# Attention stage: the rows' turns queued behind the experts' last product on VectorE, and a pause of 1024 columns ahead of the experts' down products

## The chip, the cores and the metric

The kernel runs on one core of a Trainium2 chip. The metric is the device time of one launch in microseconds (us). The engines are called PE (TensorE, matrix products), DVE (VectorE), ACT (ScalarE), POOL (GpSimd) and SP (SyncE, which here only issues transfers). Each works through its own queue in order, and semaphores order the queues among each other.

## The reference

Four residual blocks are applied to x, 8 batches of 512 rows of 256 values, all in float32: a scan block, a mixture of experts, an attention, and the same mixture again.

```python
x = x + scan(layernorm(x))         # silu(x Win), a decaying scan over the rows, Wout
x = x + ffn(layernorm(x))          # 16 routed experts, 4 chosen per row, and 2 shared experts
x = x + attention(layernorm(x))    # causal, 16 heads of 16, scores clipped to -10..10
x = x + ffn(layernorm(x))
# within ffn:
sh = jax.nn.silu(x @ sh_gate_w) * (x @ sh_up_w) @ sh_down_w
return (routed + sh).reshape(hidden_states.shape)
```

The change concerns the third block, and the shared experts and the routing of the fourth, which run beside it.

## The kernel before, in words

The kernel has four stretches. From 0 to about 366 us it runs the scan over the batches, with the routing and the shared experts of the first mixture beside it; from there to 746 us the routed experts of the first mixture, in blocks of 128 rows; from 746 to about 1260 us the attention over the batches, with the routing and the shared experts of the second mixture beside it; from there to 1672 us the routed experts of the second mixture. The change touches the third stretch alone.

That stretch is a loop over the batches b = 0 to 7 (`stretch`, with `class Attention`). The work of one pass is cut into pieces, and `beside` traces them interleaved: it always takes the next step of the piece that is furthest behind, by the share of its columns that are done; at a tie the piece that stands first. The pieces of a pass are:

- **main**, the attention of batch b: ten steps. Step n issues a burst of scores (PE, `ps_a`, L1244; three bursts ahead of its use, so that the last bursts belong to batch b+1), whose exponentials ACT takes (L1254) and whose clamps DVE makes (L1264 and L1265), and then a burst of mixing products (PE, `po_a`, L1280). After steps 2, 4, 7 and 9 DVE divides the sums and turns them (L1295 to L1305). Step 9 mixes first, and its score burst follows as a step of its own. Four output products (`py_a`, L486) end the piece. In a middle pass it has 18432 columns.
- **fill**: the projections of batch b+1 (four `pq_a` products, L1192, and four `pv_a`, L1210; 6144 columns) and, from pass 2 on, behind them the shared experts of batch b-2 (`shared_experts`; 12288 columns). These are four rounds of a gate product and an up product (`pg_m`, L1108, 1024 columns each), and four down products (`pd_m`, L1137). Of each round ACT takes a tanh (L1122), and DVE makes two products (L1123 `sig_m`, L1124 `act_m`). The down products read all four `act_m`.
- **pieces by the clock of the pass** (`timed`): a step is due at a given share of the pass. They are the norm, the scores and the choices of batch b-1's routing (the choices L656 to L700 are a long chain of small DVE instructions), the sending of routed rows (POOL), and, for batch b+2, its load, its sum (L166), its norm and its turn.

The turn of batch b+2 goes by `by_shares`: the normed rows `xn` are written to memory and read back by quarters (SP, L416 and L419), and two DVE transposes (L428, `xT_l<-xn`) make the operand of that batch's projections, which are in the next pass. Its two steps are due at `turns = (0.65, 0.85)`: the transfers at 0.65 and the transposes at 0.85.

Tracing order is not queue order. A scheduler orders each engine's queue at build time by its own model of time: an instruction that is traced later goes ahead where it is ready sooner. `tc.issue_after(ins)` takes that freedom away: what is traced within it is queued behind `ins` on the engine of `ins`, without waiting for its result.

In the last pass (b = 7) the shared experts of batch 5 are split: six steps (`HELD`) go into the pass, at an even pace worked out from `columns // 12`, and the rest goes into the piece that follows.

Of the kernel before, what the change touches and what calls it, by code (L numbers as in the profile page):

```python
# [12 lines left out]
ALU = mybir.AluOpType  # L13
# [3 lines left out]
SQ = 32  # L17
QUAD = P // SQ
B, T, D = 8, 512, 256
NT = T // P  # L20
KD = D // P
# [8 lines left out]
NSH = 2  # L30
KF = F // P
# [28 lines left out]
KB, COLS = 9, 6  # L60
HALVED = 1597463007.0
PACE = 2
SENT = 4
HELD = 6
AHEAD = 6
# [17 lines left out]
def tile_hybrid_block(  # L83
# [22 lines left out]
    nc = tc.nc  # L106
# [8 lines left out]
    def bank(shape, name: str, kind: str = "one"):  # L115
        kind = instead.get(kind, kind)
        return stage[kind].tile(shape, FP, tag=kind, name=name)
# [33 lines left out]
    def rows_of(part, b: int):  # L151
        return part[b * T : (b + 1) * T, :].rearrange("(t p) d -> p t d", p=P)
# [139 lines left out]
    steps = const.tile([P, NJ], FP, name="steps")  # L292
# [72 lines left out]
    def timed(steps, *places):  # L365


        def scaled():
            now = 0
            for place in places:  # L370
                yield place - now
                now = place
                next(steps)
            for _ in steps:
                pass

        return Piece(1, scaled())

    def spread(first: float, last: float, many: int):
        return [first + (last - first) * k / many for k in range(many)]  # L380

    def some(steps, many: int):

        for _ in range(many):
            yield next(steps)
# [3 lines left out]
            pass  # L389


    wide = []

    def turned(src, tag: str, into, copies, home=None, past=None):

# [15 lines left out]
    def by_shares(src, tag: str, into, into_rows: bool):  # L411


        rows = src()
        through = dram.tile([T, D], FP, name=f"through_{tag}")
        nc.sync.dma_start(out=through.rearrange("(t p) d -> p t d", p=P), in_=rows)  # L416
        share = rows.rearrange("p t d -> p (t d)") if into_rows else kb4(f"share_{tag}").rearrange("p t d -> p (t d)")
        for a in range(QUAD):
            nc.sync.dma_start(  # L419
                out=share[a * SQ : (a + 1) * SQ, :].rearrange("s (g c) -> s g c", g=T // SQ),  # L420
                in_=through[:, a * KD * SQ : (a + 1) * KD * SQ].rearrange("(g s) c -> s g c", s=SQ),
            )
        yield 0
        dst = work.tile([P, KD, T], FP, tag="kb4", name=f"xT_{tag}", bufs=KB)
        into(dst)
        for half in range(2):
            g = slice(half * T // SQ // 2, (half + 1) * T // SQ // 2)
            nc.vector.transpose(  # L428
                dst.rearrange("p k (g s) -> p k g s", s=SQ)[:, :, g],
                share.rearrange("p (g i k) -> p k g i", i=SQ, k=KD)[:, :, g],  # L430
            )
        yield 0

    by_both = (nc.scalar.copy, nc.vector.tensor_copy)
# [40 lines left out]
    def kb4(name: str):  # L475
        return work.tile([P, NT, D], FP, tag="kb4", name=name, bufs=KB)
# [21 lines left out]
    class Scan:  # L498
        mixture, ahead, copies, turns = 0, 1, by_scalar, (0.75, 0.79)
# [82 lines left out]
    class Route:  # L582
# [24 lines left out]
        def scores(self, shares: bool = False):  # L607
            if shares:
                yield from by_shares(
                    lambda: self.held["rows"][:, :, 0:D], self.tag, lambda xnT: self.held.update(xnT=xnT), False  # L610
                )
                yield from logits(self.i, self.b, self.tag, self.held)
                return
            yield from turned(
                lambda: self.held["rows"][:, :, 0:D],
                self.tag,
                lambda xnT: self.held.update(xnT=xnT),
                self.copies,
                past=wide if self.i == 0 and self.b == B - 2 else None,
            )  # L620
            yield from logits(self.i, self.b, self.tag, self.held)
# [31 lines left out]
    def choices(i: int, b: int, tag: str, held, paced: bool):  # L653
# [96 lines left out]
        for t in range(NT):  # L750
            for k in range(TK):
                at = t * TK + k
                if paced and at % PACE == 0:

                    pair = slice(at, at + PACE)
                    tc.keep_in_program_order(nc.scalar.copy(slots[:, pair], places[:, pair]))  # L756
# [336 lines left out]
    def shared_experts(i: int, b: int, xnT_of, tanh: bool):  # L1093

        tag = f"m{i}_{b}"

        def steps():
            xnT = xnT_of()
            acts = []
            for n in range(NSH):  # L1100
                _, g_sb, u_sb, _ = shared[n]
                act = work.tile([P, KF, T], FP, tag="kb4", name=f"act_{tag}_{n}", bufs=KB)
                acts.append(act)
                for f in range(KF):
                    pair = [bank([P, T], f"pg_{tag}_{n}_{f}_{which}") for which in range(2)]
                    for dst, w in zip(pair, (g_sb, u_sb)):
                        for k in range(KD):
                            made = nc.tensor.matmul(  # L1108
                                dst,
                                lhsT=w[:, k, f * P : (f + 1) * P],  # L1110
                                rhs=xnT[:, k, :],
                                start=(k == 0),
                                stop=(k == KD - 1),
                            )
                        wide[:] = [made]
                        if dst is pair[0]:
                            yield KD * T
                    ph, pu = pair
                    sig = work.tile([P, T], FP, tag="col", name=f"sig_{tag}_{n}_{f}", bufs=COLS)
                    if tanh:  # L1120

                        nc.scalar.activation(sig, ph, AF.Tanh, scale=0.5)  # L1122
                        nc.vector.scalar_tensor_tensor(sig, sig, 1.0, ph, ALU.add, ALU.mult)  # L1123
                        nc.vector.scalar_tensor_tensor(act[:, f, :], sig, 0.5, pu, ALU.mult, ALU.mult)  # L1124
                    else:
                        nc.scalar.activation(sig, ph, AF.Sigmoid)
                        nc.vector.tensor_mul(sig, ph, sig)
                        nc.vector.tensor_mul(act[:, f, :], pu, sig)
                    yield KD * T
            y_sb = kb4(f"ys_{tag}")  # L1130
            for half in range(2):
                py = bank([P, 2, D], f"pd_{tag}_{half}")
                for j in range(2):
                    t = 2 * half + j
                    for n in range(NSH):
                        for f in range(KF):
                            nc.tensor.matmul(  # L1137
                                py[:, j, :],
                                lhsT=acts[n][:, f, t * P : (t + 1) * P],
                                rhs=shared[n][3][:, f, :],  # L1140
                                start=(n == 0 and f == 0),
                                stop=(n == NSH - 1 and f == KF - 1),
                            )
                    yield NSH * KF * D
                nc.scalar.copy(y_sb[:, 2 * half : 2 * half + 2, :], py)

            (nc.gpsimd if b == B - 1 else nc.sync).dma_start(out=rows_of(parts[i][1], b), in_=y_sb)

        return Piece(NSH * KF * (2 * KD * T + NT * D), steps())

# [8 lines left out]
        return w_all[:, at : at + NT * D].rearrange("p (a b) -> p a b", a=rows)  # L1161

    class Attention:
        mixture, ahead, copies, turns = 1, 2, by_both, (0.65, 0.85)
        early = 2
        norms, scores, choose = (0.0, 0.12, 0.2, 0.28), (0.29, 0.45, 0.55, 0.6), (0.66, 0.95)
        last_rows, last_scores = (0.2, 0.28), (0.35, 0.38)
# [212 lines left out]
    def stretch(layer):  # L1380
# [12 lines left out]
        def turn(b: int, copies=layer.copies):  # L1393
            if i == 1 and b >= layer.ahead:
                return by_shares(lambda: xn.pop(b), f"l{i}_{b}", lambda xnT: xT.update({b: xnT}), True)
            return turned(lambda: xn.pop(b), f"l{i}_{b}", lambda xnT: xT.update({b: xnT}), copies)
# [8 lines left out]
        def experts(b: int):  # L1405
            return shared_experts(i, b, lambda: routes.pop(b).held["xnT"], i == 1)
# [37 lines left out]
        for b in range(1 if begun else 0, B):  # L1444
# [19 lines left out]
            if b > 0:  # L1464
# [7 lines left out]
                if last:  # L1472
                    pieces += [
                        timed(r.scores(), *layer.last_scores, *spread(0.5, 0.56, NT)),
                        timed(some(r.rest, PICKS), *spread(0.57, 0.67, PICKS - 1), 0.76),
                        timed(some(r.rest, 3 + SENT), 0.79, 0.81, 0.83, *spread(0.85, 1.0, SENT)),
                    ]
# [17 lines left out]
            if i == 0 and b == 2:  # L1495
# [11 lines left out]
                timed(r.norm(by_vector=True), *spread(0.0, 0.05, 2 * NT)),  # L1507
                timed(sends.pop(), *spread(0.0, 0.5, NT * TK - SENT)),
                timed(r.scores(), 0.2, 0.22, *spread(0.28, 0.33, NT)),
# [111 lines left out]
```

## Time and profile before

| | |
|---|---|
| time, median of 3 runs | 1681.23 us (1679.09 to 1684.41) |
| the profiled execution | 1674.03 us |
| its span, first to last instruction | 1672.1 us |
| PE busy in the span | 1572.9 us, 94% |
| DVE, ACT, POOL busy | 1159.7, 745.4, 758.1 us |
| attention stretch, 746 to 1260 us | PE 479.9 of 514 us busy, DVE 397.3, ACT 222.5, POOL 156.9 |
| mean granted PE clock | 0.977 |

A profile shows one execution. Times in it are counted from the first instruction. A line of the timeline gives the start, the duration, the engine, the source line, the operation and its tiles, how many instructions were merged, and in brackets for how long the engine had been idle and what it had waited for. The granted clock is the share of full speed that PE was given in a window.

### The profile page before, as it was taken

To read this page: it belongs to the slowest core of one execution; us is meant where nothing else is said; L and a number is where in the kernel's file an instruction comes from. 1 tells how busy PE (TensorE), PEld (TensorE's weight loads), DVE (VectorE), ACT (ScalarE), POOL (GpSimd) and SP (SyncE) were. 2 spreads that over 40 slices of the span, in tenths; PEclk is the share of its full clock that TensorE was granted. 3 is DMA by queue.
4 is the path that set the end of the run, shared out by engine and by line. 5 is a ranking of instruction groups with operands and counts; after the bars stand their busy time and mean duration, and the time that the engine had idled before them with its cause. 6 is when DMAs were issued, how large, how long until landed. Compare 5 with 4: busy or idle time off the path is not lost.

```text
span 1672.1 us, 34224 instructions
## 1 busy us (share of the span) xinstructions
PE 1572.9 (94%) x9992; PEld 1156.6 (69%) x9992; DVE 1159.7 (69%) x3623; ACT 745.4 (45%) x1461; POOL 758.1 (45%) x655
## 2 busy tenths in 40 slices
PE   6999996979999999999999999999787999999996
PEld 3566663659999999984444454454356999999996
DVE  7988876436677766656888978978754566666664
ACT  3222332125555555546544443444213555555553
POOL 3365663525555555550023423422552555555554
PEclk9999998989999999999999999999899999999998
DMA  5354431527777766641333423332643767777776
GB/s 166 127 192 170 135 110 60 186 75 106 107 124 122 104 99 99 99 57 42 89 93 107 121 85 117 96 96 90 210 170 72 110 113 113 137 136 136 134 135 133
DMA packets 281645, 195.31 MB, mean 117 GB/s; under 512 B 168592, under 2 KB 262064, under 8 KB 281456
## 3 DMA queue, kind: packets, MB, share of 16 engines
q1 hardware_dynamic: 228368, 119.40, 27.9%
q0 software_dynamic: 51984, 72.09, 23.9%
q8 instruction: 85, 1.39, 0.3%
q10 hardware_dynamic: 1104, 1.57, 0.3%
q14 instruction: 104, 0.85, 0.2%
HBM read 89.71 MB, written 103.23 MB: 115 GB/s over the span
## 4 chain that ended last, share of the span: by engine, by line
PE 38%; DVE 9%; DMA 3%; issue 1%; ACT 1%; another core or an unknown queue 0%; DVEq 0%; POOLq 0%; SPq 0%; ACTq 0%
PE ph L994 13%; PE pyr L1025 6%; PE ps_a L1244 4%; PE pd_m L1137 3%; DMA part<-rows 3%; PE pq_a L1192 2%; PE po_a L1280 2%; PE pg_m L1108 2%; PE py_a L486 2%; PE pv_a L1210 1%; DVE w_all L1264 1%; DVE w_all L1265 1%; DVE act_m L1124 1%; ACT w_all L1254 1%; DVE sig_m L1123 1%
## 5 line engine op out<-in xcount | busy, mean ns | idle before, releaser
L1035 POOL DMA_INDIRECT part<-rows x272 | 426.3, 1567 | 339.7 <-ACT rows L1034 252.3
L759 POOL DMA_INDIRECT xg<-sorted_m,slots_m x256 | 258.6, 1010 | 293.7 <-ACT slots_m L756 78.0
L994 PEld LDWEIGHTS ph<-rows,gate 128*128 128x128 f32 x2160 | 277.8, 191 | 33.4 <-ACT rows L977 21.6
L994 PE MATMUL ph<-rows,gate 128*128 128x128 f32 x2160 | 291.5, 278 | 1.9 <-ACT rows L977 1.9
L994 PE MATMUL ph<-rows,up 128*128 128x128 f32 x2160 | 285.3, 275 | 0.0
L1025 PE MATMUL pyr<-w_all,rows 128*128 x1088 | 279.2, 380 | 0.0
L967 DVE COPY up<-w_all 128x512 f32 x270 | 118.8, 441 | 211.4 <-PE ph L994 191.6
L994 PEld LDWEIGHTS ph<-rows,up 128*128 128x128 f32 x2160 | 262.9, 192 | 0.0
L967 ACT COPY gate<-w_all 128x512 f32 x270 | 166.5, 618 | 122.3 <-DVE up L967 55.7
L1254 ACT ACTIVATE w_all<-ps_a 128x1024 f32<-128x1024 f32 x160 | 155.2, 1021 | 108.5 <-PE ps_a L1244 101.0
L1025 PEld LDWEIGHTS pyr<-w_all,rows 128*128 128x128 f32 x1088 | 186.9, 192 | 14.3
L1034 ACT ACTIVATE rows<-pyr,gain 128x256 f32<-128x256 f32 x272 | 128.9, 474 | 80.9 <-PE pyr L1025 60.1
L1002 ACT ACTIVATE rows<-ph 128x256 f32<-128x256 f32 x272 | 104.6, 384 | 114.3 <-PE ph L994 99.5
L1004 DVE TENSOR_TENSOR rows<-ph,rows 128x256 f32<-128x256 f32 x272 | 115.1, 423 | 31.7 <-ACT rows L1002 27.7
L1005 DVE TENSOR_TENSOR rows<-ph,rows 128x256 f32<-128x256 f32 x272 | 115.2, 424 | 26.2 <-issue 0.9
L1137 PE MATMUL pd_m<-sd_sb,act_m 128*128 128x256 f32 x512 | 122.8, 386 | 7.8 <-DVE act_m L1124 7.7
L1108 PE MATMUL pg_m<-xT_m,sg_sb 128*128 128x512 f32 x256 | 123.3, 604 | 0.0
L1108 PE MATMUL pg_m<-xT_m,su_sb 128*128 128x512 f32 x256 | 122.5, 600 | 0.0
L1137 PEld LDWEIGHTS pd_m<-sd_sb,act_m 128*128 128x128 f32 x512 | 96.4, 192 | 31.3 <-DVE act_m L1124 9.3
L1244 PE MATMUL ps_a<-w_all 32*128 32x384 f32 (+3 forms) x1024 | 104.7, 475 | 14.0 <-ACT w_all L1254 13.9
L1264 DVE SCALAR_TENSOR_TENSOR w_all<-w_all,causal 128x512 f32<-128x512 f32 (+1 forms) x160 | 91.8, 574 | 33.3 <-ACT w_all L1254 31.2
L1244 PEld LDWEIGHTS ps_a<-w_all 32*128 32x128 f32 x1024 | 45.2, 190 | 69.6 <-ACT w_all L1254 39.1
(213 smaller groups left out, 1960.3 us busy)
## 6 DMA issues: line engine op xcount, KB each, us to landing
rows<-xg SPq DMA_DIRECT2D x720, 32.0 KB
rows<-xg SPq DMA_DIRECT2D x92, 134.0 KB
part<-x SPq DMA_DIRECT2D x16, 512.0 KB
part<-ys_m SPq DMA_DIRECT2D x14, 512.0 KB
sum<-part SPq DMA_DIRECT2D x14, 512.0 KB
w_all<-in_L_ffn_gate_w_dram SPq DMA_DIRECT2D x27, 256.0 KB
w_all<-in_L_ffn_up_w_dram SPq DMA_DIRECT2D x27, 256.0 KB
w_all<-in_L_ffn_down_w_dram SPq DMA_DIRECT2D x27, 256.0 KB
```

Source lines behind the costliest of these rows:

```text
L759: nc.gpsimd.indirect_dma_start(out=xg[i], out_offset=bass.IndirectOffsetOnAxis(ap=slots[:, at : at + 1], axis=0), in_=rows[:, t, :], in_of ...
L967: copy(here, w_all[:, bass.ds(held[n][0] + half * KD * F, KD * F)])
L994: nc.tensor.matmul(ph[s][:, f * P : (f + 1) * P], lhsT=both[s][:, k * F + f * P : k * F + (f + 1) * P], rhs=rows[:, ROW + k * P : ROW + (k ...
L1004: nc.vector.tensor_mul(act, ph[0], act)
L1005: made = nc.vector.tensor_mul(act, ph[1], act)
L1025: nc.tensor.matmul(py, lhsT=act[:, f * P : (f + 1) * P], rhs=w_all[:, bass.ds(w + 2 * KD * F + f * D, D)], start=(f == 0), stop=(f == KF - 1),
L1034: nc.scalar.mul(y, py, gain[:, TK : TK + 1])
L1035: acc = nc.gpsimd.indirect_dma_start(out=parts[i][n % 2], out_offset=bass.IndirectOffsetOnAxis(ap=rows[:, D + 2 * TK : D + 2 * TK + 1].bit ...
L1108: made = nc.tensor.matmul(dst, lhsT=w[:, k, f * P : (f + 1) * P], rhs=xnT[:, k, :], start=(k == 0), stop=(k == KD - 1),)
L1137: nc.tensor.matmul(py[:, j, :], lhsT=acts[n][:, f, t * P : (t + 1) * P], rhs=shared[n][3][:, f, :], start=(n == 0 and f == 0), stop=(n == ...
L1244: nc.tensor.matmul(ps[j // 2][:, j % 2, col : col + n], lhsT=k_sb[w][r, o, c * P : (c + 1) * P], rhs=q_sb[r, o, c * P : T], start=True, st ...
L1254: nc.scalar.activation(es[two], ps[two], AF.Exp, scale=ATT_SCALE)
```

## The change

Three edits, all in the attention stretch:

- `shared_experts` pauses for 1024 columns (`BREAK`) between its last `act_m` and its first down product, where it uses tanh (the second mixture). In the pause it traces nothing, and `beside` counts the columns as done. The piece's columns grow from 12288 to 13312, so each of its other steps stands at a smaller share of the fill.
- It keeps its latest `act_m` in `acted`, and the two transposes of the turn (`into_rows`, which is the turn of a later batch) are queued behind it on DVE, once there is one (from pass 2 on).
- The transposes are due at 0.96 of the pass in place of 0.85.

```diff
+BREAK = 1024
...
-    wide = []
+    wide, acted = [], []
...
-            nc.vector.transpose(
-                dst.rearrange("p k (g s) -> p k g s", s=SQ)[:, :, g],
-                share.rearrange("p (g i k) -> p k g i", i=SQ, k=KD)[:, :, g],
-            )
+            with tc.issue_after(acted[-1].ins) if into_rows and acted else nullcontext():
+                nc.vector.transpose(
+                    dst.rearrange("p k (g s) -> p k g s", s=SQ)[:, :, g],
+                    share.rearrange("p (g i k) -> p k g i", i=SQ, k=KD)[:, :, g],
+                )
...
-                        nc.vector.scalar_tensor_tensor(act[:, f, :], sig, 0.5, pu, ALU.mult, ALU.mult)
+                        acted[:] = [nc.vector.scalar_tensor_tensor(act[:, f, :], sig, 0.5, pu, ALU.mult, ALU.mult)]
...
+            if tanh:
+                yield BREAK
             y_sb = kb4(f"ys_{tag}")
...
-        return Piece(NSH * KF * (2 * KD * T + NT * D), steps())
+        return Piece(NSH * KF * (2 * KD * T + NT * D) + tanh * BREAK, steps())
...
-        mixture, ahead, copies, turns = 1, 2, by_both, (0.65, 0.85)
+        mixture, ahead, copies, turns = 1, 2, by_both, (0.65, 0.96)
```

## The prediction

> **What bounds the kernel now.** I read the page's busy shares first, then busy time by stretch, then PE's waits in the attention stretch, then its timeline around each wait. In that stretch PE is busy for 480 of 514 us, so only a stall of PE or a change in its clock moves the end. Its waits from 746 to 1160 us (in total, how often, the longest):
>
> ```profile
> PE pd_m L1137 <- DVE act_m L1124: 7.7, 4, 1.9
> PE ps_a L1244 <- ACT w_all L1254: 4.9, 9, 1.4
> PE py_a L486 <- DVE oT_a L1305: 1.4, 2, 0.7
> ```
>
> The first line is what the change is about: in passes 2 to 5, the down products wait for the experts' last product on DVE. Pass 2, PE:
>
> ```profile
> 893.82 1.98 PE L1108 MATMUL pg_m<-xT_m,sg_sb 128*128 128x512 f32 x4
> 895.64 1.88 PE L1108 MATMUL pg_m<-xT_m,su_sb 128*128 128x512 f32 x4
> 897.45 1.07 PE L1280 MATMUL po_a<-w_all,v_a 128*32 128x128 f32 x16
> 898.45 1.56 PE L1137 MATMUL pd_m<-sd_sb,act_m 128*128 128x256 f32 x6
> 901.93 0.70 PE L1137 MATMUL pd_m<-sd_sb,act_m 128*128 128x256 f32 x2 [1.92 <-DVE act_m L1124]
> ```
>
> Six of the first eight down products need only the first three `act_m`; the fourth is wanted at 901.93 - 1.92 = 900.01. On DVE at that time:
>
> ```profile
> 897.85 0.71 DVE L428 STREAM_TRANSPOSE xT_l<-xn 128x512 f32<-128x512 f32 x1
> 898.48 0.65 DVE L1264 SCALAR_TENSOR_TENSOR w_all<-w_all,causal 128x512 f32<-128x512 f32 x1
> 899.04 0.42 DVE L1265 TENSOR_SCALAR w_all<-w_all 128x512 f32<-128x512 f32 x1
> 899.38 0.71 DVE L428 STREAM_TRANSPOSE xT_l<-xn 128x512 f32<-128x512 f32 x1
> 900.01 1.06 DVE L689 CAST sorted_m<-which_m 128x16 f32<-128x16 uint32 x1
> 900.05 1.02 DVE L1123 SCALAR_TENSOR_TENSOR sig_m<-sig_m,pg_m 128x512 f32<-128x512 f32 x1
> 901.19 0.69 DVE L1124 SCALAR_TENSOR_TENSOR act_m<-sig_m,pg_m 128x512 f32<-128x512 f32 x1
> ```
>
> No line carries an idle time: DVE is late, not waiting. It works from 873.88 to 901.88 with one hole of 0.32 us. Both turns stand ahead of the last product, and each takes 0.63 us to the next start. So does a cast that takes 1.06 us, where its like in pass 6 takes 0.15; it falls on POOL's memset of the value tile (899.96 to 901.03).
>
> After the stall PE's clock is not always whole (the column before the last two is the granted clock):
>
> ```profile
> 902.00:906.00 4.00, 4.00 (x29) 3.06 (x30) 3.62 (x9) 2.20 (x3) 0.00 (x0) 1.00 0.01 2
> 962.50:966.50 4.00, 3.83 (x21) 2.56 (x22) 2.75 (x8) 1.10 (x2) 0.00 (x0) 0.62 0.00 0
> ```
>
> The same stall leaves the clock whole in passes 2 and 4 and drops it in passes 3 and 5. There the score burst that follows takes 2.02 and 2.09 us in place of 1.15, and the next down products 2.75 and 2.57 in place of 1.99: 1.63 + 1.52 = 3.15 us. From one such last product to the next it is 60.74, 62.38 and 60.74 us, and the 62.38 holds pass 3's drop, which agrees. The most that can be had at this place is 7.7 + 3.15 = 10.8 us, 0.64% of the time.
>
> **Part 1: the turns go behind the last product.** 2 x 0.63 = 1.26 us leave the queue ahead of it. The next projections need the operand at 914.54, some 12 us after the old end of the last product, so the turns stay hidden; lost cover would cost that wait at the head of the next pass. Behind `act_m` come the shares of the attention: the turned output ends at 904.51 and the output products start at 905.47. One turn fits into that 0.96 us, and two would cost 0.3 a pass if nothing else moved back. No transfer moves: the step at 0.65 stays, and with it SP's queue and POOL's. Each `xn` is freed some 4 us later; the sum that a later load feeds is 40 us away.
>
> **Part 2: the turns due at 0.96.** From pass 2 on, the new edge already holds them. In passes 0 and 1 there is no `act_m` yet; their turns (800.21, 846.29) run just ahead of the output products' two waits of 0.63 and 0.74. Those could go (-1.4), but in the old due order these turns stood behind the shares too and ran early because they were ready. I take 0.
>
> **Part 3: the pause.** In pass 2 to 6 the fill grows from 18432 to 19456 columns beside a main piece of 18432. Before, most steps of the fill tie with a step of main and come second. Now they come a little earlier and go first: the first gate product goes ahead of the burst of step 4, the second up ahead of step 6, the third up ahead of step 7, the fourth gate ahead of step 8. The first down product moves from 0.778 to 0.789 and stays behind step 9's mixing and ahead of the next score burst (0.833). So a score burst comes to stand between the last gate and the last up product, but between the last up and the first down product there remains the one mixing of 1.07 us.
>
> What that does to DVE: step 4's burst starts 1.82 us later (one gate product, 873.66 to 875.48), and its clamps can start at 875.70 in place of 873.88. Into the hole that this leaves goes the first `sig_m` (0.59). The work up to the last product is 28.00 - 0.32 - 1.26 - 0.59 = 25.83 us, so it ends at 875.70 + 25.83 = 901.53, which is 1.5 us after 900.01; without the cast's 0.91 us it is 0.6. If the rest of the choices (L692 and L700, 0.76) goes ahead as well, because the last product is ready later than they are, it is 2.3. If the choices from L570 on (3.7 us) go behind it, it is 0. **I take a stall of 1.3 in place of 1.92: 4 x -0.6 = -2.4 us** (from -7.7 to +1.4).
>
> **Clock**: a stall of 1.45 us (835.39) was followed by a clock of 0.57, waits of 0.6 and 0.7 by none below 1.00. I let one of two drops go: -1.6 (from -3.15 to +3.15, where the other two passes drop as well).
>
> [...]
>
> **The bursts' own wait.** Two bursts share two buffers, which ACT's two exponentials free. At 785 us a burst ended at 786.35 and the next was held until 2.07 us later, over a mixing of 1.07: stalls of 0.16 + 0.42. Between the bursts of steps 2 and 3 there stood a mixing (0.57) and a `pq_a` (1.98); now there stands a `pv_a` of 0.93. The second starts 1.5 us after the first, runs a quarter (0.27) and waits 0.3 us: 5 passes, **+1.5** (from 0 to 5 x 0.58 = 2.9).
>
> **Pass 6** has no turns. Its last product ended at 1145.88 and was wanted at 1144.63 + 1.56 = 1146.19. With step 6's clamps 1.91 us later (behind the second up product), the 14.7 to 15.5 us of DVE work that follow end at 1146.3 to 1147.2: +0.5 (from 0 to 1.7). Pass 7 changes its order by one product; I take 0.
>
> [...]
>
> **Sum**: -2.4 - 1.6 + 1.5 + 0.5 = -2.0 us. The profiled execution took 1674.03 (span 1672.1 and 1.93 around it), so 1672.0 for one like it; it lies 7.2 under the median of the runs, 1681.23, which becomes **1679.2**.
>
> **Rivals.**
>
> A, the forecast: the stalls shrink and the new order gives most of it back. For it: DVE has no hole from 873.88 to 901.88, so taking out 1.26 us can't remove 1.92 by itself. 1676.2 to 1686.3 (0.3% of 1681.23 is 5.0 us, about what a measurement of this kernel can tell from no change). Chance 0.47.
>
> B, the last product gets clear: the choices go behind it or the cast misses the memset, all four stalls and both drops go. -7.7 - 3.15 + 1.5 = -9.4: 1671.8. With the waits of passes 0 and 1 gone, 1670.4. For it: without turns, pass 6 was on time by 0.31 us. Against: its cast was 0.9 us shorter, and the new order delays the clamps. Chance 0.35.
>
> C, **slower**: DVE's backlog grows. The mechanism is the score bursts that now stand behind a product: their clamps reach DVE 1.8 us later and all stand ahead of the last product. It decides once the work ahead of that product grows by more than the 1.26 us taken out. At 2.3 us a stall: 4 x 0.36 = +1.4; drops in the other two passes, +3.15; pass 6, 1.7 and a drop of 1.6; bursts, 2.9: +10.7, 1691.9; half of it, 1686.6. Chance 0.18.
>
> That the change doesn't do what it says (the edge holds what was harmless) would give A's middle without the gain, +2.0: 1683.2, within A.
>
> **Chances**: faster by over 0.3% is B, 0.35; within, A, 0.47; slower, C, 0.18. The range goes from B with the early waits gone (1670.4) to C a little past its half (1688): 1670.4 to 1688.
>
> **What would show it.** PE's wait for `act_m` in passes 2 to 5: gone (B), 0.6 to 1.5 (A), over 1.9 (C). A wait for ACT ahead of step 3's burst of about 0.3 in passes 2 to 6. The gate product ahead of the burst of step 4, and both turns behind the last `act_m`. The granted clock in the 4 us after the first down products. The cast's duration, and what now falls on the memset. I am wrong if the length of a pass changes by over 1.5 us, or if the time moves in a stretch that the change doesn't touch.

## The result and the profile after

The changed kernel takes 1684.95 us (median of 20 runs) beside 1680.76 for the kernel before on the same chip: a ratio of 1.0025, 95% interval 1.0017 to 1.0033. It is slower by 4.2 us, where 2.0 us less had been forecast. On another chip, where the kernel before takes 1634 us, the ratio is 1.0041 (1.0029 to 1.0053).

The two profiled executions lie 12.9 us apart (1687.18 and 1674.03), more than the medians do: the one of before is 7 us under its median, and 3.4 us of the difference lie ahead of the attention, where the code is the same. From there to the start of pass 1 it takes 60.93 us in place of 59.51: the granted clock fell to 0.62 and 0.53 on the way (766 to 770 and 770 to 774 us), as it does in another execution of the kernel before (e5 below: 0.72 and 0.50). So the traces are compared by stretch. PE's waits in the attention, changed kernel, 746 to 1165 us (in total, how often, the longest):

```profile
PE pd_m L1141 <- DVE act_m L1126: 7.1, 5, 1.6
PE ps_a L1248 <- ACT w_all L1258: 4.9, 9, 1.4
PE pg_m L1110 <- issue: 1.6, 4, 0.4
PE py_a L488 <- DVE oT_a L1309: 0.7, 1, 0.7
```

Line numbers are two to four higher than in the kernel before: `act_m` is L1126, `pd_m` L1141, `ps_a` L1248, `oT_a` L1309. The wait for the last product is still there and has one more place, pass 6. A wait of 0.4 is new in each of passes 2 to 5; the trace of the same kernel on another chip (e10 below) names `act_m` on DVE as what ended it. Pass 2 on PE:

```profile
871.13 1.65 PE L1248 MATMUL ps_a<-w_all 32*128 32x128 f32 x16
...
892.33 0.65 PE L632 MATMUL pl_m<-xT_m,rw_sb 128*32 128x128 f32 x16
893.36 1.99 PE L1110 MATMUL pg_m<-xT_m,su_sb 128*128 128x512 f32 x4 [0.39 <-issue]
...
898.83 1.15 PE L1248 MATMUL ps_a<-w_all 32*128 32x128 f32 x16
...
901.34 1.98 PE L1110 MATMUL pg_m<-xT_m,su_sb 128*128 128x512 f32 x4
903.25 1.07 PE L1284 MATMUL po_a<-w_all,v_a 128*32 128x128 f32 x16
904.25 1.56 PE L1141 MATMUL pd_m<-sd_sb,act_m 128*128 128x256 f32 x6
907.44 0.70 PE L1141 MATMUL pd_m<-sd_sb,act_m 128*128 128x256 f32 x2 [1.62 <-DVE act_m L1126]
```

The order is the predicted one: a score burst stands ahead of the last up product, and only the mixing of 1.07 us between it and the down products. The burst of step 3 (first line) takes 1.65 us; in the kernel before it is this line:

```profile
865.43 1.15 PE L1244 MATMUL ps_a<-w_all 32*128 32x128 f32 x16
```

From its start to the next product's it is 1.59 us (871.13 to 872.72) in place of 1.08 (865.43 to 866.51), so 0.51 more. DVE ahead of the last product:

```profile
904.64 0.67 DVE L1268 SCALAR_TENSOR_TENSOR w_all<-w_all,causal 128x512 f32<-128x512 f32 x1
905.23 0.42 DVE L1269 TENSOR_SCALAR w_all<-w_all 128x512 f32<-128x512 f32 x1
905.57 0.17 DVE L691 CAST sorted_m<-which_m 128x16 f32<-128x16 uint32 x1
905.65 0.68 DVE L1268 SCALAR_TENSOR_TENSOR w_all<-w_all,causal 128x512 f32<-128x512 f32 x1
906.25 0.55 DVE L1269 TENSOR_SCALAR w_all<-w_all 128x512 f32<-128x512 f32 x1
906.72 0.67 DVE L1126 SCALAR_TENSOR_TENSOR act_m<-sig_m,pg_m 128x512 f32<-128x512 f32 x1
```

The turns are gone from here and the cast is short, and still the product is late, because DVE stood idle further ahead. These are its holes in pass 2:

```profile
879.38 0.69 DVE L1125 SCALAR_TENSOR_TENSOR sig_m<-sig_m,pg_m 128x512 f32<-128x512 f32 x1 [2.07 <-ACT sig_m L1124]
880.94 0.69 DVE L1268 SCALAR_TENSOR_TENSOR w_all<-w_all,causal 128x512 f32<-128x512 f32 x1 [0.87 <-ACT w_all L1258]
890.53 0.41 DVE L471 TENSOR_SCALAR xn<-x,mv_l,rstd_l 128x256 f32<-128x256 f32 x1 [1.23 <-POOL rstd_l L466]
```

Step 4's clamps (the second of these lines) start 24.36 us into the pass (880.94 - 856.58); before, it was 22.15 (873.88 - 851.73):

```profile
873.88 0.69 DVE L1264 SCALAR_TENSOR_TENSOR w_all<-w_all,causal 128x512 f32<-128x512 f32 x1 [2.44 <-ACT w_all L1254]
```

Counted from the start of its pass, the last `act_m` begins 0.68 us later than before (50.14 against 49.46), though turns and cast no longer stand ahead of it. The wait is shorter only because PE asks for it 0.96 us later (49.24 against 48.28).

A pass without any stall would take 60.74 - 1.92 = 58.82 us. Adding what is seen, 58.82 + 1.62 + 0.39 + 0.51 = 61.34; passes 2 to 5 take 61.39, 61.41, 61.39 and 61.35. Before, they took 60.74, 62.38, 60.74 and 62.33, two of them with a drop of the clock (to 0.62 and 0.57 in the 4 us after the wait). There is none after (4 us from the end of the wait, passes 2 and 3):

```profile
907.50:911.50 4.00, 4.00 (x29) 3.06 (x30) 3.80 (x9) 2.19 (x3) 1.06 (x1) 1.00 0.00 0
969.00:973.00 4.00, 4.00 (x29) 3.06 (x30) 3.90 (x9) 2.29 (x3) 1.05 (x1) 1.00 0.00 0
```

So passes 2 to 5 gained 0.65 us in all, pass 6 lost 1.48 (58.55 to 60.03), and from the start of pass 7 to the first product of the second routed experts it takes 127.84 us in place of 121.74. The kernels of e1 and e3 below, which have the old order there, take 123.99 and 124.61 on the same chip, and e2, which has the new order, 128.67. By these single executions 3.2 to 3.9 of the 6.1 us belong to the change and the rest to the execution. What this last stretch waits for, on DVE:

```profile
DVE sig_m L1125 <- issue: 17.1, 1, 17.1
DVE xT_m L409 <- remote: 5.3, 1, 5.3
```

"issue" and "remote" name no releaser in the profile. In the trace of before, the same stretch has such holes of 7.8, 5.3 and 4.7 us, at other instructions.

### The profile page after: what moved, and what is told of

Read it like the earlier page. It is cut to its first block, busy times and chain, and to the rows that moved or that the text cites. A ratio compares the mean times of both kernels' runs of the same rounds, so it can differ in the third digit from the quotient of the medians.

```text
span 1685.0 us, 34223 instructions
## 1 busy us (share of the span) xinstructions
PE 1583.9 (94%) x9992; PEld 1159.9 (69%) x9992; DVE 1154.8 (69%) x3623; ACT 744.4 (44%) x1461; POOL 763.0 (45%) x655
## 3 DMA queue, kind: packets, MB, share of 16 engines
q8 instruction: 85, 1.39, 0.3%
q10 hardware_dynamic: 1104, 1.57, 0.3%
## 4 chain that ended last, share of the span: by engine, by line
PE 39%; DVE 8%; DMA 3%; issue 1%; ACT 1%; another core or an unknown queue 1%; POOL 0%; DVEq 0%; SPq 0%; POOLq 0%; ACTq 0%
PE ph L996 13%; PE pyr L1027 6%; PE ps_a L1248 4%; PE pg_m L1110 3%; PE pd_m L1141 3%; DMA part<-rows 3%; PE po_a L1284 3%; PE pq_a L1196 2%; PE py_a L488 2%; PE pv_a L1214 2%; DVE w_all L1268 1%; DVE w_all L1269 1%; DVE act_m L1126 1%; ACT w_all L1258 1%
## 5 line engine op out<-in xcount | busy, mean ns | idle before, releaser
L761 POOL DMA_INDIRECT xg<-sorted_m,slots_m x256 | 265.1, 1036 | 283.7 <-issue 77.1
L1141 PE MATMUL pd_m<-sd_sb,act_m 128*128 128x256 f32 x512 | 124.6, 390 | 7.1 <-DVE act_m L1126 7.1
L1248 PE MATMUL ps_a<-w_all 32*128 32x384 f32 (+3 forms) x1024 | 108.1, 476 | 11.0 <-ACT w_all L1258 10.0
L1141 PEld LDWEIGHTS pd_m<-sd_sb,act_m 128*128 128x128 f32 x512 | 97.1, 193 | 30.2 <-DVE act_m L1126 9.1
L1248 PEld LDWEIGHTS ps_a<-w_all 32*128 32x128 f32 x1024 | 46.9, 189 | 68.1 <-ACT w_all L1258 27.8
```

What stands on the lines that cost most here:

```text
L761: nc.gpsimd.indirect_dma_start(out=xg[i], out_offset=bass.IndirectOffsetOnAxis(ap=slots[:, at : at + 1], axis=0), in_=rows[:, t, :], in_of ...
L1141: nc.tensor.matmul(py[:, j, :], lhsT=acts[n][:, f, t * P : (t + 1) * P], rhs=shared[n][3][:, f, :], start=(n == 0 and f == 0), stop=(n == ...
L1248: nc.tensor.matmul(ps[j // 2][:, j % 2, col : col + n], lhsT=k_sb[w][r, o, c * P : (c + 1) * P], rhs=q_sb[r, o, c * P : T], start=True, st ...
```

## Experiments

The theory (O): the turns behind the last product gain on their own, and the pause takes it back, since its columns turn ties and so move products ahead of score bursts. Rivals: the turns bring nothing (E); the loss lies behind pass 5 (T); the pause's length costs it (P). Runs e1 to e4 were made where the kernel before takes the result's 1680.8 us (called the first chip here), e5 to e8 and e13 to e16 on a second chip, e9 to e12 on a third; each ratio is to the kernel before on the same chip (medians 1680.8, 1634.6 to 1635.1, and 1634.4 us). The two other chips agree with each other and not with the first; more on that below.

**e1, the turns alone.** Against the changed kernel:

```diff
-            if tanh:
-                yield BREAK
...
-        return Piece(NSH * KF * (2 * KD * T + NT * D) + tanh * BREAK, steps())
+        return Piece(NSH * KF * (2 * KD * T + NT * D), steps())
```

> Without the pause; the turns stay bound and due at 0.96. PE's order is that of before; on DVE the two turns stand behind the output's turn, and the cast comes one clamp earlier. Theory O (the pause's changed order of products gives back what the turns win): the last product comes 1.26 us earlier for the turns, and 0.9 more if the cast now misses the memset: PE's wait in passes 2 to 5 falls from 1.92 us to 0.7 or less, and with it the drops of the clock; -5 to -9 us, a ratio to before of 0.995 to 0.997. Rival E (moving the turns brings nothing, because something else then ends last on DVE): the wait stays at 1.6 to 1.9 us and the ratio is 0.999 to 1.001.

Ratio 0.9934 (0.9921 to 0.9948), 10.4 us by the medians, more than expected. The wait falls to 0.36 ("issue" here; e9 and e12 name `act_m`):

```profile
902.38 1.56 PE L1139 MATMUL pd_m<-sd_sb,act_m 128*128 128x256 f32 x6
904.30 0.70 PE L1139 MATMUL pd_m<-sd_sb,act_m 128*128 128x256 f32 x2 [0.36 <-issue]
```

Passes 2 to 5 take 59.14 to 59.18 us with no drop. E falls. PE's order here is that of before, and so is DVE's up to the turns and the cast. The turns run at 909.11, some 5 us behind the last product and behind the output's turn. No run has them due at 0.96 without the edge in passes 2 to 5, so it isn't shown which of the two puts them there. Pass 1 has a wait of 2.08 us for the turned output and a granted clock of 0.67 behind it (46.93 us in place of 45.49); in e12, the same kernel on another chip, the wait is 0.74 as before and the pass takes 45.54.

**e2, the pause alone.** The edge is taken out (`with nullcontext():`) and the turns are due at 0.85.

> The pause alone: turns unbound and due at 0.85 as before. Theory O: DVE still has the 1.26 us of turns ahead of the last product and gets its clamps later, so PE's wait in passes 2 to 5 grows to 2.5 to 2.9 us and a pass to 62 us or more: ratio to before 1.004 to 1.007. Rival E: like the changed kernel, 1.002 to 1.003.

Ratio 1.0088 (1.0073 to 1.0104). The wait is 3.03 to 3.07 us, more than the 2.5 to 2.9 expected, and the clock dropped behind three of four (to 0.58, 0.63 and 0.67 in the 4 us after; passes of 64.5 us; 62.85 without). So -10.4 for the turns and +14.6 for the change (1684.95 - 1670.38) over e1: the pause is what costs.

**e3, the pause for passes 2 to 5 only.**

```diff
-            if tanh:
+            if tanh and b < B - 4:
                 yield BREAK
```

(and the same condition in the columns)

> The changed kernel with the pause only for the experts of batches 0 to 3, which run in passes 2 to 5; pass 6, pass 7 and the piece behind it have the columns of before. Theory T (the loss is behind pass 5: pass 6 took 1.48 us longer, and pass 7 with what follows 6.1 us longer in the profiled executions): the ratio falls to 0.998 to 1.000. Theory O alone, with the tail as noise between executions: only pass 6's 1 to 1.5 us go, ratio 1.001 to 1.002.

Ratio 1.0003 (0.9994 to 1.0012). Passes 2 to 5 as in the changed kernel (61.41 to 61.43), pass 6 58.56. That is between the two forecasts: 3.3 us of the loss lie behind pass 5, by the medians; the intervals leave some 2 us either way. The other 11.3 us over e1 are mostly passes 2 to 5 (9.0 us in the two traces, 245.68 and 236.68).

**e4, the pause without added columns.** The `yield BREAK` stays, the piece's columns are 12288 again.

> The changed kernel, but the pause's 1024 columns are not added to the columns of the piece: the steps ahead of the pause keep their places, and the first down product comes behind the last score burst, so a burst of 1.1 us more stands between the last up product and the first down product. Theory O: no product moves ahead of a score burst, DVE's clamps come as before, and the wait for the last product goes altogether: -8 to -11 us, ratio 0.9935 to 0.995; a wait of the output products for their turned operand of up to 0.5 us a pass may take 2 us of it. Rival E (DVE late whatever stands where): wait of 0.5 to 0.8 left, ratio 0.997 to 0.999.

Ratio 0.9959 (0.9945 to 0.9974). All ties stand as before, and a score burst really comes between last up and first down product. The wait for the last product is gone, but the output products, now a down product sooner, wait 1.00 to 1.07 us for their turned operand, where up to 0.5 was expected: passes of 59.62 to 59.69, longer than e1's, and the ratio misses the expected one. So even a burst in that place brings nothing once the turns are moved.

**e8, that pause with the turns left as before.**

> The pause without added columns, and the turns left as in the kernel before (unbound, due at 0.85): the score burst stands between the last up and the first down product, DVE's order is that of before but for the turns' absence of any edge. Theory D (DVE's queue is late, and PE's order decides only where the wait shows): the wait for the last product goes, and the output products wait 1.9 to 3.3 us for their turned operand instead, because it comes no earlier and they now come a down product sooner: ratio 0.999 to 1.003. Rival S (the burst covers the wait): 1.1 us a pass gained, ratio 0.996 to 0.998.

Ratio 0.9997 (0.9988 to 1.0006). Pass 2 of e8:

```profile
878.98 0.70 PE L1141 MATMUL pd_m<-sd_sb,act_m 128*128 128x256 f32 x2 [0.83 <-DVE act_m L1126]
...
881.61 0.70 PE L488 MATMUL py_a<-w_att,oT_a 128*128 128x256 f32 x2 [1.50 <-DVE oT_a L1309]
```

0.83 + 1.50 in place of 1.92, and no gain clear of the noise: what PE does meanwhile only moves the wait along DVE's queue (theory D, though it had the wait for the last product gone altogether).

**e5, the kernel before again.**

> The kernel before once more, for its trace alone. If the 12.9 us between the two profiled executions are partly the executions' own (code that is the same took 3.4 us longer in the scan's stretch, and the first execution of before lies 7 us under its median), the first product of the attention starts at 749 to 751 us in place of 746.73, and pass 7 with what follows, up to the second routed experts, takes 124 to 125 us in place of 121.74. If before is really faster there, both repeat within 0.5 us. The drops of the clock may lie in other passes; the waits of 1.92 us repeat in passes 2 to 5.

It ran on the second chip: 1637.42 us, one run. The waits of 1.92 and the lengths of passes 1 to 6 repeat within 0.03 us, with the drops in the same passes 3 and 5. So the passes are the program's. From pass 7 to the second routed experts it takes 104.20 us where the first chip took 121.74, without holes that name no releaser, so the expectation can't be judged on it. The first chip itself answers a part of it: in e1 to e4 the first product of the attention starts at 748.81 to 749.99, so the 746.73 of before was that execution's own.

**e6, a pause of one column** (`BREAK = 1`).

> The changed kernel with a pause of 1 column in place of 1024: nothing is left of the pause but that each of the fill's steps stands a hair earlier than main's, so the ties turn; only the third gate product stands where it stood before. Theory O (the turned ties cost the time, not the pause): ratio 1.000 to 1.003, the wait for the last product in passes 2 to 5 is 1.2 to 1.9 us. Rival P (the pause's length, which pushes products together, costs it): ratio 0.993 to 0.996 as with the turns alone.

Ratio 1.0053 (1.0039 to 1.0066). The ties alone cost as much as the whole change (1.0041 on the third chip) and P falls. The wait (2.69) is longer than expected: POOL's memset runs from 878.97 to 880.04, and the cast beside it takes 1.68 us, the clamps behind it 1.61 and 1.27, see e16.

**e13 to e15, one group of ties each**, on top of e1. The edit gives one step a column less and the next one more, so that the named ties turn and the others stay; e13:

```diff
-                        yield KD * D
+                        yield KD * D - (b > 2 and h == 1 and j == 1)
...
-                            yield KD * T
+                            yield KD * T + (tanh and b < B - 3 and n + f == 0)
```

> The turns alone, with one tie turned in passes 2 to 6: the first gate product goes ahead of step 4's scores, all else on PE as before. Theory G (this tie, as the prediction had it: the clamps of step 4 reach DVE 1.8 us later and its backlog ends later): the wait for the last product is 1.0 to 1.8 us in passes 2 to 5 in place of 0.36, passes 59.8 to 60.7, ratio to before 0.9965 to 0.999. Rival L (the late ties, those of the second up and the fourth gate product, do it): wait 0.36, passes 59.2, ratio as the turns alone, 0.9934 to 0.9945.

> The turns alone, with one tie turned in passes 2 to 6: the fourth projection product goes ahead of step 2's scores, so the score bursts of steps 2 and 3 come closer. The changed kernel's trace has a score burst of 1.65 us in place of 1.08 there. Expected by it: 0.57 us a pass, passes 59.75, the wait for the last product unchanged at 0.36; ratio 0.001 to 0.002 above the turns alone, 0.995 to 0.997. If the longer burst is not this tie's doing: no change.

> The turns alone, with two ties turned in passes 2 to 5: the second up product ahead of step 6's scores and the fourth gate product ahead of step 8's. Theory G: they matter less than the first one, wait 0.4 to 0.9 us, ratio within 0.001 of the turns alone. Rival L: wait 1.0 to 1.8 us, passes 59.8 to 60.7, ratio 0.9965 to 0.999.

e13: 0.9994 (0.9985 to 1.0003), wait 2.28. e14: 0.9985 (0.9976 to 0.9994), wait 0.36. e15: 0.9987 (0.9978 to 0.9996), wait 1.76. Over the turns alone (0.9945, but on the third chip) that is about 8, 6.5 and 7 us. These prices hold more than the ties. One clamp ahead of the last product takes 1.68 us in e13 and 1.39 in e15 in place of 0.42, beside POOL's memset (e16); without that the waits would be, by estimate, 2.28 - 1.26 = 1.0 and 1.76 - 0.97 = 0.8 us, where e1 has 0.36. So the early tie and the late ones both lengthen the wait; which is the dearer isn't shown. In e13 the clamps start 23.87 us into the pass, 1.72 later than in e1. In e14 the burst that comes too close is held far longer than I had it; e14's pass 2:

```profile
841.67 1.14 PE L1246 MATMUL ps_a<-w_all 32*128 32x512 f32 x8
842.75 0.64 PE L1282 MATMUL po_a<-w_all,v_a 128*32 128x256 f32 x8
843.97 2.05 PE L1246 MATMUL ps_a<-w_all 32*128 32x128 f32 x16 [0.59 <-ACT w_all L1256]
```

0.59 idle and 0.9 more in the burst itself: 1.5 us. The changed kernel has a projection between the two and loses 0.51. The costs of the groups don't add up to that of all together: e14's burst is held longer than the changed kernel's, and e13 and e15 each carry what e16 is about.

**e7 and e16, the memset moved.** POOL's memset of the value tile is queued behind the next norm; e7 in the kernel before, e16 in the changed one:

```diff
-                nc.gpsimd.memset(v_sb, 1.0)
...
+                with tc.issue_after(rooted[-1].ins) if rooted else nullcontext():
+                    nc.gpsimd.memset(v_sb, 1.0)
                 for h in range(2):
...
-            nc.gpsimd.tensor_tensor(rstd, rstd, neg_half, ALU.pow)
+            rooted[:] = [nc.gpsimd.tensor_tensor(rstd, rstd, neg_half, ALU.pow)]
```

> The kernel before, but POOL's memset of the value tile is queued behind the norm of the next pass, some 12 us later; nothing else moves. Theory M (the cast takes 1.06 us because the memset runs beside it): the cast takes 0.17 us, the last product comes 0.9 us earlier, the wait in passes 2 to 5 is 1.0 us: -3.6 us and with fewer drops of the clock up to -6; ratio 0.9965 to 0.998. If the cast is slow by itself in this place, nothing changes: 0.999 to 1.001. What the memset meets now must show a longer row in its place, or none if DVE is idle there.

e7: 0.9968 (0.9957 to 0.9980). The cast takes 0.13 us, but the wait falls only to 1.55. The cast (1.06) and the `sig_m` behind it (1.02) overlapped in the record and ended together; from the cast's start to that of `act_m` it was 1.18, and is now 0.83. Of the gain of 5.2 us (0.0032 x 1635), 1.5 are this (4 x 0.37), and 3.2 that no drop followed a wait of 1.55 where before there were two of 1.6. In passes 2 to 6 the memset now runs beside three instructions of the norm, which take 1.88 us together (1.06 in the kernel before), and no pass grows by it. In pass 1 it meets a clamp (1.09 us in place of 0.55), and that pass takes 46.08 us in place of 45.49.

> The changed kernel with POOL's memset queued behind the norm of the next pass, 12 us or more later. Theory M (the memset on the clamp makes the difference between 1.5 and 2.75 us): no clamp of 1.68 us, the wait is 1.5 to 1.6 us in all four passes on any chip, passes 61.3 each without a drop, ratio to before 0.999 to 1.001 (on a chip where the changed kernel has 1.004). If the two lengths have another cause, 2.75 stays in some passes and the ratio at 1.003 to 1.004.

e16: 1.0006 (0.9997 to 1.0016), waits of 1.62, 1.63, 1.62, 1.51, passes of 61.30 to 61.41. M holds.

**e9 to e12, on the third chip.** e9 binds the turns behind the last turn of the output:

```diff
-                    nc.vector.transpose(held["oT"][:, o, :], both.rearrange("p q c -> p (q c)"))
+                    acted[:] = [nc.vector.transpose(held["oT"][:, o, :], both.rearrange("p q c -> p (q c)"))]
```

(no pause, and `act_m` no longer sets `acted`)

> The turns alone (no pause, due at 0.96), but bound behind the last turn of the attention's output in every pass in place of the experts' last product, so in passes 0 and 1 too. Against the turns alone, the one turn that still ran ahead of the output's turn in pass 0 and pass 1 goes behind it: the output products' wait in pass 1 falls by 0.6 us, pass 0's stays at none to 0.1, and if a wait of 2.08 us drops the clock and one of 1.4 does not, 1.4 us more: 0.6 to 2.0 us under the turns alone, ratio to before 0.992 to 0.993 where the turns alone have 0.9934. If it brings nothing, the same ratio.

> The changed kernel once more, for a second trace beside others on one chip. Theory O: passes 2 to 5 take 61.4 us each again, pass 6 60.0. Where DVE and PE show holes that nothing explains in the last pass and behind it (the chip of the first traces), the tail takes 125 to 128 us and the ratio is 1.002 to 1.003; on a chip without these holes (tail 104 us in two kernels there) the tail costs nothing, and the ratio is what the passes give: 1.48 of pass 6 less 0.65 of passes 2 to 5, 1.000 to 1.001.

> The pause for batches 0 to 3 only, once more beside the changed kernel on one chip. If its gain over the changed kernel (1.0003 against 1.0025, 3.3 us) was pass 6's 1.48 and the holes of the tail, it keeps 1.5 us of gain on any chip, and 3 on the chip with holes.

> The turns alone, once more, beside the other three. Passes 2 to 5 are a matter of the program, not of the chip: 59.18 us each, 2 x 1.56 + 2 x 3.15 = 9.4 us less than before in these four, and pass 1 up to 1.4 longer where its wait drops the clock: 0.9935 to 0.995 on either chip.

e9: 0.9926 (0.9914 to 0.9939), 1622.18 us beside 1634.39, the fastest version, though its interval still touches e12's. Its wait in pass 1 is 0.26 us where e12's is 0.74. e12: 0.9945 (0.9932 to 0.9958), with e1's passes of 59.14 to 59.18. e10, the changed kernel: 1.0041, where 1.000 to 1.001 was expected: that missed. Its tail costs nothing (103.30 us, before 104.20 on the second chip), but three of its four waits are 2.75 us and one 1.50, and passes 2 to 6 take 310.5 us where e5 has 304.7: 5.8 of the 6.7 us (0.0041 x 1634). The wait of 0.39 has its releaser here:

```profile
865.83 1.99 PE L1110 MATMUL pg_m<-xT_m,su_sb 128*128 128x512 f32 x4 [0.39 <-DVE act_m L1126]
```

In pass 2 the clamp ahead of the last product meets the memset (e10, DVE and POOL):

```profile
878.71 1.68 DVE L1269 TENSOR_SCALAR w_all<-w_all 128x512 f32<-128x512 f32 x1
880.31 0.67 DVE L1126 SCALAR_TENSOR_TENSOR act_m<-sig_m,pg_m 128x512 f32<-128x512 f32 x1
```

```profile
879.03 1.07 POOL L1191 MEMSET v_a<- 128x1148 f32 x1
```

1.68 in place of 0.42. In pass 4 the indirect transfer ahead of the memset took 1.57 us in place of 0.98, the memset started 0.57 after the last product had, and the clamp took 0.42: up to that clamp the two passes agree row by row. On the first chip the memset came late in all four passes of the changed kernel:

```profile
907.69 1.06 POOL L1191 MEMSET v_a<- 128x1148 f32 x1 [1.12 <-remote]
```

e11: 1.0032 (1.0021 to 1.0042). It lies 0.0009 (1.5 us) under e10, with overlapping intervals, and its median is 0.45 above e10's; the expected gain isn't shown. In the traces pass 6 has its 58.56 again (59.97 in e10), but all four waits are 2.73 to 2.75 us here and the clock dropped behind two of them (the score burst that follows takes 1.40 and 1.81 us in place of 1.15).

## Why the prediction was wrong

The sum was -2.0 us, and it is +4.2. The step that failed is the price of the pause's new order, in two groups of terms. Passes 2 to 5 were to give -2.8 (-2.4 for the stall, -1.6 for the clock, +1.2 for four of the five bursts) and gave -0.65. Passes 6 and 7 were put at 0.8 (0.5, a burst of 0.3, and nothing for pass 7) and cost 3.3 by the medians (e3), with the holes of this chip in it. Set against the turns alone (e1), the pause costs 14.6 us. By parts:

- **The bound** was right: DVE's backlog ahead of the last product, and PE waiting for it. e1 and e8 show it from both sides.
- **Part 1, the turns**: right in kind. They stayed hidden, no later wait appeared in passes 2 to 5, and with the shorter cast they close the wait but for 0.36 (1.92 - 1.26 - 0.35 = 0.31). The **cast** was put at 0.91 us and is worth 0.36 (e7): I took one row's length for the delay, where two rows overlapped. That 1.26 us "can't remove 1.92 by itself" was true, and yet with the cast it nearly did.
- **Part 2, the turns at 0.96**: the wait of pass 0 went and that of pass 1 stayed, -0.6 where 0 was taken. Whether "the new edge already holds them" from pass 2 on wasn't tried, see e1.
- **Part 3, the pause**: the order and the later clamps were right (2.2 us, put at 1.82). The wait was put at 1.3 and is 1.62. The backlog was summed as if DVE would stay full behind that hole; it then waited 1.23 us for POOL's `rstd_l`, which the sum doesn't have. -1.2 in place of -2.4.
- **Not seen at all**: the third up product now stands right behind the router's product and waits 0.39 for the `act_m` of the round before (it ends at 893.31, the product starts at 893.36): 4 x 0.39 = 1.6.
- **The bursts**: put at 0.3 a pass, measured 0.51 in five passes: 2.5 in place of 1.5, near the upper bound of 2.9.
- **The clock**: no drop after, -3.15 in place of -1.6, on this chip; in e10 one drop remains.
- **Pass 6**: 1.48 in place of 0.5, with a wait of 0.65 for the last product.
- **Pass 7**, "changes its order by one product; I take 0", failed most: 3.2 to 3.9 us on this chip by single traces, 1.8 by the medians (3.3 less pass 6's 1.48), with some 2 us either way. There the pieces' columns were scaled by 13312/12288 too, and several products moved. That the order costs where the chip has its holes, and nothing on the third chip, is what these traces show; which of the moved instructions costs it on the first chip was not tried.

Passes 0 and 2 to 6 give -0.6 - 0.65 + 1.48 = +0.2 and the tail 3.2 to 3.9: 3.4 to 4.1, measured 4.2. With the tail by the medians it would be 2.0, so how the last 2 us are shared stays open. Behind the single terms stands one choice: the three edits were summed into one, and a net of nearly nothing was taken for small parts. They were -10.4 and +14.6. Rival B had the right size for the turns alone, rival C the right mechanism for the pause ("the score bursts that now stand behind a product").

The prediction asked for "what now falls on the memset". In passes 2 to 5 of the changed kernel the memset lengthened no row on the first chip (the transpose beside it takes 0.72 us); on the third it cost the clamp 1.26 us. The rows that the memset made longer were of CAST and TENSOR_SCALAR, and what stood right behind them; a transpose (0.71) and `act_m` (0.69) beside it were not (e9, e12, e14). In pass 2 of e10 the clamp's row begins 0.32 us ahead of the memset's (878.71 and 879.03) and ends 0.29 behind its end (880.39 and 880.10). How the memset holds DVE up isn't shown.

## What to carry to other kernels

- Work that is interleaved by shares has ties, and columns added to one piece turn nearly all of them: e6 does it with one column. To hold one instruction back, move or bind that one (e9), and leave the shares alone.
- Where an engine's queue is late, take work out from ahead of the instruction that is waited for (e1: a wait of 0.36 us in place of 1.92). Putting other work of the waiting engine in between only moved the wait here (e8: 0.83 + 1.50), and putting products ahead of the bursts that feed the late engine lengthened it (1.62 in e16 against 0.36 in e1).
- Run each edit by itself before judging the sum: two large effects of opposite sign look like a small one.

## What the runs showed of the hardware

- **The same program takes 46 us longer on the first chip** (1681 and 1635 us). The passes are equal to 0.03 us. The difference lies from 200 to 366 us (PE busy 137.5 us there, 158.7 on the second chip) and from pass 7 on (121.74 and 104.20 us), in holes for which the profile names no releaser. What they are stays open, and so does why the memset comes 1.1 to 1.2 us later there in the changed kernel, e2 and e3, and not in e1 and e4.
- **Whether the clock drops depends on more than the wait's length.** Behind 17 waits of 1.50 to 1.64 us for the last product (the changed kernel, e3, e7, e16, one in e10) it never dropped (1.00 in the 4 us after each); behind those of 1.76 it did in three of four (e15), of 1.92 in two of four, of 2.28 in one of four (e13), of 2.7 in five of eleven (e6, e10, e11), of 3.05 in three of four (e2). Where it dropped, it was 0.57 to 0.71 in the 4 us after (before, e2, e6, e10, e13 and e15). Passes 2 and 3 of e15, with the same wait:

```profile
878.20:882.20 4.00, 4.00 (x22) 2.64 (x23) 2.89 (x7) 1.51 (x2) 0.00 (x0) 0.60 0.00 0
940.00:944.00 4.00, 4.00 (x29) 3.06 (x30) 3.61 (x9) 2.16 (x3) 0.00 (x0) 1.00 0.00 0
```

- **One memset of 1.07 us costs DVE from nothing to 1.26 us**, by what it meets and when; in one kernel both happen within one execution (e10: 1.26 in passes 2, 3 and 5, nothing in pass 4).
